# Two transpositions of a top-k attention layer moved from TensorE to VectorE's 32x32 block transposes and transfers

## The chip, the cores and the metric

The program runs on one core of one Trainium2 chip. The metric is the device time of one execution, in microseconds (us). Before the change it is 2491.27 us, the median of three runs (2487.93 to 2491.57). The core's engines are TensorE (PE, with its weight loads PEld), VectorE (DVE), ScalarE (ACT), GpSimd (POOL) and SyncE (SP), each with an instruction queue of its own that it works through in order. Sixteen DMA engines carry the transfers that SP, ACT and POOL issue.

## The reference

Two layers in float32, on 8 images (batches) of 512 channels and 1024 positions (tokens):

```python
# layer 0: group norm, 8-head attention over 1024 tokens, projection, residual
x = _L0_conv_ref(x, ...)
# layer 1
q, kk, v = wq @ xf, wk @ xf, wv @ xf                # [B, 512, 1024]
importance = nan_to_num(sum(xf * xf, axis=1))       # one number per token
_, idx = top_k(importance, 256)
q_sel, k_sel, v_sel = q[idx], k[idx], v[idx]        # 256 rows of 512
q_sel, k_sel = layer_norm(q_sel), layer_norm(k_sel)
attn = softmax(clip(q_sel @ k_sel.T * 512**-0.5, -80, 80))
out = v.at[idx].set(attn @ v_sel)                   # 256 tokens are replaced
return x + wo @ out
```

## The kernel before

Layer 0 fills the first four fifths of the time. Its output, the input of layer 1, lies in DRAM (`x1_dram`). Layer 1 works image by image. Wo is multiplied into Wv ahead of it (`w["vo"]`), so a token's value is its row of the output already. For an image `b` the steps are:

- `load_x1` (L204): four transfers of 512 KB bring the image, channels on the partitions.
- `row` (L245), `square` (L250), `keep_row` (L255), `put` (L258): for each of 8 blocks of 128 tokens TensorE transposes four 128x128 tiles into PSUM. ScalarE sums the squares into the importance, copies the rows to SBUF and issues their transfer to `x_dram`.
- `finite` (L261), `spread_row` (L269), `imp` (L277): the importance, a number per partition, is spread over all partitions by 8 TensorE transposes and two copies of ScalarE.
- `count` (L281), `place` (L328), `pick` (L336), `holder` (L344), `who` (L353): VectorE counts for each token how many are ahead of it (its place), and a small product finds which token holds each of the 256 places.
- `vo` (L306), `vkeep` (L314), `vput` (L325): 32 products of 128 tokens by 512 channels (8 blocks times 4 channel tiles) give all values. ScalarE copies them to the tile `V` and issues their transfer to `v_dram`.
- `gather` (L359, steps getx and getv), `selt`, `selk`, `qk` (L401), `stats`, `root`, `normal` (L424), `normt`, `scale` (L449), `score`, `clip`, `exp`, `inv`, `probt`, `probk`, `att`, `attk` (L521), `attput` (L527): the attention of the 256 chosen tokens, down to a transfer to `a_dram`. Only the last image takes `vsel` and `vselk` (L372 to L383), which compute the chosen values again rather than gather them.
- `fetch` (L533): eight indirect transfers of POOL write the attended rows over those tokens of `V` that were chosen; an index past 255 moves nothing.
- `back` (L546), `residual` (L541), `add` (L555): TensorE transposes `V` back, 32 tiles of 128x128 per image; VectorE adds the image's x, read once more from DRAM, and SP sends the sum out in eight transfers of 256 KB.

The order of all this is written out by hand in the strings `BATCH` (one round, repeated) and `END` (the last rounds), one word per step: `vo3` is `vo(b, 3)`, each `+` is one image ahead of the round's, each `-` one behind. Every engine's queue gets its instructions in the order of that list, those that issue transfers too. `EARLY` names the steps of image 0 that are done in layer 0's last units, through `token_rows` (L904), `token_values` (L916), `importance` (L1096), `count_first` (L1106), `begin_layer1` (L1135) and `finish` (L1157).

Of the kernel before, what the change touches and what calls it, by code (L numbers as in the profile page):

```python
# [9 lines left out]
F32 = mybir.dt.float32  # L10
BF16 = mybir.dt.bfloat16
I32 = mybir.dt.int32
AF = mybir.ActivationFunctionType
ALU = mybir.AluOpType
# [4 lines left out]
P = 128  # L19
# [20 lines left out]
BLOCKS = 2 * HALF // BLOCK  # L40
ET = mybir.EngineType
# [17 lines left out]

BATCH = """  # L60
vkeep6- square1 inv-- put4 put2 holder- add3--- keep1 square2 back4--- att0-- att1-- who-
row6 put1 row0 add4--- row7 keep0 back7--- square0 row3 keep6 attk0-- put0 square3 vo0 row5
vput7- square6 getx- vput4- attk1-- keep3 square7 square5 add7--- vput5- back6--- keep7
finite vo1 attput-- add6--- vput0- vkeep0 keep5 selt1- selt0- spread1 spread0 fetch1-- imp1 imp0
count2 fetch0-- put6 count5 vo3 count7 vkeep1 selk1- selk0- qk1- count6 count3 qk0-
fetch5-- qk2- vput6- vput3- stats0- stats1- vput2- qk3- root0- stats2- root2- fetch2-- norm0-
vkeep3 put5 norm2- vput1- root1- vo4 vkeep4 stats3- fetch3-- norm1- vo2 root3- back0--
fetch6-- fetch4-- norm3- fetch7-- normt1- normt0- count4 vkeep2 add0-- put3 put7 back5--
normt2- normt3- scale2- scale3- row4+ add5-- back1-- scale1- count0 back2-- vo5 scale0-
count1 square4+ keep4+ place score0- score1- clip- back3-- vo6 vkeep5 pick0 add1-- exp- vo7  # L70
getv- add2-- pick1 row2+ probt- vkeep7 row1+ probk- keep2+
"""
END = """
vput2-- put4- vkeep6-- row3- add3---- square2- holder-- att1--- back4---- row0- who-- inv---
put2- row7- square1- keep1- attk1--- att0--- getx-- square3- keep3- keep0- keep7- put1- put3-
put7- row5- back6---- attk0--- row6- square7- back7---- square6- add4---- square0- square5-
keep5- keep6- put0- vput5-- vo1- put5- selt1-- finite- vkeep1- spread1- add6---- add7----
selk1-- selt0-- spread0- imp1- imp0- attput--- count1- vo0- row6 row2 vput7-- selk0-- count6-
keep6 keep2 row1 square2 count0- count2- vput6-- count7- row0 count3- vkeep0- square1 keep1
put1 vput1-- qk0-- row7 qk1-- put6- square0 put2 stats1-- qk3-- stats0-- count5- put6 keep7  # L80
square6 vo7- put7 root1-- vput1- fetch5--- row4 root0-- norm0-- qk2-- keep0 stats3--
fetch3--- count4- vo6- place- square4 vkeep7- keep4 norm1-- square7 root3-- stats2-- row3
vput0- vkeep6- vo4- normt1-- root2-- norm3-- normt0-- vput0-- row5 keep3 fetch1--- vput4--
vput3-- norm2-- vkeep4- scale1-- normt2-- put3 normt3-- scale0-- fetch2--- pick1- scale2--
square5 square3 keep5 put5 vo2- fetch0--- pick0- holder- finite spread0 scale3-- put4 vkeep2-
imp0 getv-- fetch6--- spread1 who- imp1 score0-- back2--- count4 score1-- fetch7--- count2
clip-- exp-- count3 vput2- back0--- count7 getx- vput4- count6 put0 add0--- vo3- count0
fetch4--- probt-- vkeep3- probk-- inv-- add2--- att0-- att1-- attk1-- attk0-- selt1- selt0-
selk1- selk0- attput-- count5 fetch6-- count1 qk3- place stats3- pick0 back3--- back4---
vput6- add4--- root3- pick1 back1--- qk2- fetch4-- qk0- fetch0-- norm3- add3--- fetch2--  # L90
vput7- back7--- stats2- stats0- holder fetch3-- fetch1-- qk1- who vput3- add7--- root0-
root2- add1--- back5--- norm2- getx add5--- back6--- vo5- normt3- stats1- norm0- fetch7--
root1- fetch5-- norm1- normt2- vkeep5- add6--- normt0- normt1- back2-- scale0- scale3-
scale2- back5-- back7-- vput5- add2-- back1-- add1-- selt1 back6-- back3-- scale1- add7--
add5-- score0- add6-- back0-- selt0 score1- selk1 add3-- clip- selk0 qk2 exp- stats2 back4--
qk1 probt- probk- stats1 getv- add0-- qk0 qk3 att1- root2 root1 norm2 norm1 stats0 inv-
stats3 add4-- root0 attk1- vo1 att0- root3 norm3 vkeep1 norm0 attk0- normt3 normt2 normt0
attput- scale3 normt1 fetch5- scale0 scale1 fetch7- fetch6- vo0 vkeep0 scale2 score1 fetch1-
score0 clip vsel1 fetch4- vo3 exp vselk1 vsel0 vselk0 probt fetch0- probk fetch2- vkeep3 vo6
att1 inv fetch3- att0 vo7 vkeep6 vo2 back0- attk1 back2- back4- attk0 vkeep7 back3- attput  # L100
vkeep2 add3- add0- back5- vo4 fetch7 fetch3 vo5 vkeep4 add2- back1- back7- fetch2 back6-
fetch0 fetch1 add4- add1- fetch6 add7- add5- back2 back4 add4 add6- back0 back6 fetch4 vkeep5
add0 fetch5 back3 back7 add2 back1 add6 back5 add3 add7 add1 add5
# [15 lines left out]
def attention_then_topk_attention(  # L119
# [23 lines left out]
    x1_dram = [dram.tile([P, CT, N], F32, tag=f"x1d{b}", name=f"x1d{b}") for b in range(B)]  # L143
# [25 lines left out]

    xp = ctx.enter_context(tc.tile_pool(name="xp", bufs=1))  # L170
# [6 lines left out]
    a_dram = [dram.tile([TOP, C], F32, tag=f"sa{b}", name=f"sa{b}") for b in range(B)]  # L177

# [25 lines left out]
    def load_x1(b):  # L204

        if b % 2 and b < B - 1:
            x1[b] = [qk_tile(tag, i, f"x1_{b}_{tag}{i}") for tag in "qk" for i in range(2)]
        else:
            if b == B - 1:
                t = pools["x2"].tile([P, CT, N], F32, tag="x2", name=f"x1_{b}")  # L210
            else:
                t = xp.tile([P, CT, N], F32, tag="x1", name=f"x1_{b}")
            x1[b] = [t[:, c, :] for c in range(CT)]
        for c in range(CT):
            nc.sync.dma_start(x1[b][c], x1_dram[b][:, c, :])

    def load_layer1():

        t = wide.tile([P, CT, 3 * C], F32, tag="w3", name="w1")
        for i, (name, src) in enumerate((("q", wqT), ("k", wkT), ("vo", None))):  # L220
            w[name] = t[:, :, ts(i, C)]
        load_x1(0)
        for name, src in (("q", wqT), ("k", wkT)):
            nc.sync.dma_start(w[name], src.rearrange("(k p) o -> p k o", p=P))
# [18 lines left out]


    def row(b, j):  # L245
        pt = bank(("pt", b, j))
        for c in range(CT):
            nc.tensor.transpose(pt[:, ts(c, P)], x1[b][c][:, ts(j, P)], ident)

    def square(b, j):  # L250
        norm = get("r1", ("norm", b), [P, NB], "norm", 2)
        sq = keep_pool.tile([P, C], F32, tag="sq", name=f"sq_{b}_{j}", bufs=1)
        nc.scalar.activation(sq, tiles["pt", b, j], AF.Square, accum_out=norm[:, j : j + 1])

    def keep_row(b, j):  # L255
        nc.scalar.copy(get("r1", ("xT", b, j), [P, C], "xT", XT), tiles["pt", b, j])

    def put(b, j):  # L258
        nc.scalar.dma_start(x_dram[b][ts(j, P), :], tiles["xT", b, j])

    def finite(b, _):  # L261
# [4 lines left out]
        col = get("r1", ("col", b), [P, NB], "col", 2)  # L266
        nc.vector.scalar_tensor_tensor(col, norm, F32_MAX, fin, ALU.is_le, ALU.mult)

    def spread_row(b, j):  # L269
        pi = bank(("pi", b, j))  # L270
        for i in range(NB // 2):
            nb = j * (NB // 2) + i
            nc.tensor.transpose(
                pi[:, ts(i, P)], tiles["col", b][:, nb : nb + 1].broadcast_to([P, P]), ident
            )

    def imp(b, j):  # L277
        t = get("rp", ("imp", b), [P, N], "imp", 1)
        nc.scalar.copy(t[:, ts(j, HALF)], tiles["pi", b, j])
# [26 lines left out]
    def vo(b, j):  # L306
        pv = bank(("pv", b, j))
        for k in range(CT):
            nc.tensor.matmul(  # L309
                pv, x1[b][k][:, ts(j, P)], w["vo"][:, k, :],  # L310
# [3 lines left out]
    def vkeep(b, j):  # L314
        if ("V", b) not in tiles:
            if b % 3:
                tiles["V", b] = pools["up"].tile([P, NB, C], F32, tag=f"V{b % 3}", name=f"V_{b}")
            else:
                tiles["V", b] = xp.tile([P, CT, N], F32, tag="x0", name=f"V_{b}").rearrange(
                    "p c (a n) -> p (c a) n", n=C  # L320
                )
        V = tiles["V", b]
        nc.scalar.copy(V[:, j, :], tiles["pv", b, j])

    def vput(b, j):  # L325
        nc.scalar.dma_start(v_dram[b][ts(j, P), :], tiles["V", b][:, j, :])

    def place(b, _):  # L328
# [4 lines left out]
        nc.vector.tensor_copy(get("rp", ("at", b), [P, NB], "at", 4, mybir.dt.uint32), t)  # L333
# [38 lines left out]
    def vsel(b, rb):  # L372

        pv = bank(("sv", b, rb))
        for k in range(CT):
            nc.tensor.matmul(  # L376
                pv, tiles["selT", b][:, k, ts(rb, P)], w["vo"][:, k, :],
                start=(k == 0), stop=(k == CT - 1),
            )
# [894 lines left out]
```

## Time and profile before

| what | us |
|---|---|
| median of three runs | 2491.27 |
| the profiled execution, its own time | 2489.56 |
| its span, first to last instruction | 2487.9 |
| busy time in the span: PE, DVE, ACT, POOL | 2437.7, 1963.3, 1414.8, 1160.7 |
| start of layer 1's first tile on PE (image 1's rows, L248) | 2020.7 |
| last matrix instruction of image 0's to 7's values (L309), end | 2475.4 |
| data moved from 2020 us on | 84.49 MB |

A profile line of the groups reads: line of the code, engine, operation, output<-inputs by the program's names, shapes, count; then the group's busy time and the mean of one in ns; then the engine's idle time before it. PE's instructions are pipelined and a single one's duration overlaps the next one's; what one costs is read from a run of them in the chain of waits, which lists what ended last as start, duration, engine, tile, line and count. A 128x512 product in float32 is two instructions.

### The profile page before, as it was taken

The numbers are of one execution on the slowest core, as the hardware profiler recorded it, in microseconds if no ns is written. First come the engines' busy times: TensorE is split into PE (matmuls) and PEld (weight loads), VectorE is DVE, ScalarE is ACT, GpSimd is POOL, SyncE is SP. The second block draws the span as 40 slices with busy tenths as digits, with TensorE's granted clock in tenths as the row PEclk, the third lists the DMA queues.
The fourth block names the chain that finished last, engine by engine and source line by source line (L and its number), as shares of the span: only waits on it lengthen the run. The fifth ranks groups of instructions, "written<-read, shape, count | busy, mean of one in ns | idle before, by whom it ended". The sixth has DMA issues, their size and how long they took to land. (4 is left out here: it accounts for less than half of the span.)

```text
span 2487.9 us, 27088 instructions
## 1 busy us (share of the span) xinstructions
PE 2437.7 (98%) x9164; PEld 1076.4 (43%) x9164; DVE 1963.3 (79%) x2946; ACT 1414.8 (57%) x1828; POOL 1160.7 (47%) x557
## 2 busy tenths in 40 slices
PE   7999999999999999999999999999999999999998
PEld 3434444444444444444444444444433345555554
DVE  4789987998898889888988898888777566666683
ACT  2567755665666566655765676567656533333421
POOL 0555644665465555545664565455555501111122
PEclk9999999999999999999999999999999999999999
DMA  3002011111211121112011201111213343566553
GB/s 142 15 26 73 30 56 51 69 35 56 84 31 43 56 79 41 43 60 77 26 47 56 77 26 49 59 39 35 89 52 106 123 161 136 209 211 240 188 198 106
DMA packets 108234, 205.24 MB, mean 82 GB/s; under 512 B 19114, under 2 KB 19370, under 8 KB 108096
## 3 DMA queue, kind: packets, MB, share of 16 engines
q1 hardware_dynamic: 82432, 159.95, 19.0%
q10 hardware_dynamic: 18144, 31.48, 3.4%
q0 software_dynamic: 7520, 12.09, 1.7%
q8 instruction: 72, 1.18, 0.2%
q14 instruction: 66, 0.54, 0.1%
HBM read 146.29 MB, written 69.73 MB: 87 GB/s over the span
## 5 line engine op out<-in xcount | busy, mean ns | idle before, releaser
L1014 POOL TENSOR_TENSOR es<-es,e 128x1024 f32<-128x1024 f32 x384 | 912.0, 2375 | 30.1
L955 ACT COPY e<-sc 128x1024 f32<-128x1024 f32 x512 | 505.6, 1013 | 389.4 <-PE sc L947 241.3
L1006 DVE TENSOR_TENSOR e<-e,ns 128x1024 f32<-128x1024 f32 x512 | 594.0, 1212 | 2.0 <-ACT ns L1002 2.0
L1014 POOL TENSOR_TENSOR es<-e,e 128x1024 f32<-128x1024 f32 x64 | 152.0, 2375 | 884.8 <-ACT e L1009 884.8
L1009 ACT ACTIVATE e<-e 128x1024 f32<-128x1024 f32 x512 | 529.1, 1055 | 31.6 <-DVE e L1006 9.8
L961 DVE TENSOR_TENSOR high<-sc,high 128x1024 f32<-128x1024 f32 x384 | 468.9, 1221 | 90.0 <-ACT e L955 50.3
L947 PE MATMUL sc<-q,k 64*128 64x512 f32 x2048 | 510.4, 616 | 5.3 <-ACT e L955 3.2
L1022 PE MATMUL av<-e,v 128*64 128x512 f32 x2048 | 469.4, 600 | 3.5 <-ACT e L1009 2.0
L750 PE MATMUL g<-x,wqkv 128*128 128x512 f32 x992 | 458.8, 605 | 3.4 <-ACT v L780 1.7
L947 PEld LDWEIGHTS sc<-q,k 64*128 64x128 f32 x2048 | 175.3, 185 | 283.6 <-issue 151.3
L750 PEld LDWEIGHTS g<-x,wqkv 128*128 128x128 f32 x992 | 178.3, 189 | 274.8 <-issue 229.9
L1022 PEld LDWEIGHTS av<-e,v 128*64 128x64 f32 x2048 | 136.1, 137 | 320.6 <-issue 257.5
L771 PE MATMUL g<-wqkv,x 128*128 128x256 f32 x976 | 227.0, 386 | 1.3 <-DVE pb L834 1.3
L789 PE MATMUL g<-o,wp 128*128 128x512 f32 x456 | 210.9, 605 | 0.8
L771 PEld LDWEIGHTS g<-wqkv,x 128*128 128x128 f32 x976 | 180.4, 190 | 69.7 <-issue 43.3
L1051 DVE RECIPROCAL rs<-rs 128x256 f32<-128x256 f32 x64 | 112.1, 1751 | 68.4 <-ACT rs L1045 68.4
L534 POOL DMA_INDIRECT V<-sa,at x64 | 64.2, 1003 | 155.2 <-DMA sa<-att 52.7
L789 PEld LDWEIGHTS g<-o,wp 128*128 128x128 f32 x456 | 81.9, 189 | 118.2 <-issue 91.3
L309 PE MATMUL b_pv<-w,x 128*128 128x512 f32 x256 | 114.1, 592 | 0.0
L405 PE MATMUL b_pp<-w,selT 128*128 128x512 f32 x256 | 112.5, 593 | 0.8 <-ACT selT L396 0.7
L961 DVE TENSOR_TENSOR high<-sc,e 128x1024 f32<-128x1024 f32 x64 | 78.1, 1220 | 37.5 <-ACT e L955 37.5
L363 POOL DMA_INDIRECT sel<-sx,who x16 | 16.1, 1007 | 191.0 <-DMA out_dram<-y 72.1
(177 smaller groups left out, 1993.6 us busy)
## 6 DMA issues: line engine op xcount, KB each, us to landing
nb<-negd SPq DMA_DIRECT2D x128, 256.0 KB
x<-in_x_dram SPq DMA_DIRECT2D x32, 512.0 KB
ri<-rsd SPq DMA_DIRECT2D x128, 128.0 KB
sx<-xT ACTq DMA_DIRECT2D x64, 256.0 KB
xr<-in_x_dram SPq DMA_DIRECT2D x58, 256.0 KB
x1d<-xr SPq DMA_DIRECT2D x58, 256.0 KB
sv<-V ACTq DMA_DIRECT2D x56, 256.0 KB
y<-x1d SPq DMA_DIRECT2D x48, 256.0 KB
```

Of the source, the lines that this page charges most:

```text
L309: nc.tensor.matmul(pv, x1[b][k][:, ts(j, P)], w["vo"][:, k, :], start=(k == 0), stop=(k == CT - 1),)
L405: nc.tensor.matmul(pp, tiles["selT", b][:, k, ts(rb, P)], w["qk"[which]][:, k, :], start=(k == 0), stop=(k == CT - 1),)
L750: nc.tensor.matmul(pq, wqkv[:, k, ts(ot, P)], hs[b][:, k, ts(hf, HALF)], start=(k == 0), stop=(k == CT - 1),)
L771: nc.tensor.matmul(pv[:, ts(j, 2 * P)], hs[b][:, k, ts(2 * part + j, P)], wqkv[:, k, 2 * C + hm * 2 * P : 2 * C + (hm + 1) * 2 * P], start ...
L789: nc.tensor.matmul(po, wp[:, k, ts(mt, P)], os[b * NPAIR + k][:, ts(hf, HALF)], start=(k == 0), stop=(k == CT - 1),)
L947: nc.tensor.matmul(sc[:, hh, :], ks[p][r, ts(j, P)], qs[p][r, ts(hf, HALF)], start=True, stop=True,)
L955: nc.scalar.copy(raw[t, j], banks["s", t, j])
L961: nc.vector.tensor_tensor(high[t], banks["s", t, j], raw[t, 0] if j == 1 else high[t], ALU.max)
L1006: nc.vector.tensor_tensor(raw[t, j], raw[t, j], high[t], ALU.add)
L1009: nc.scalar.activation(raw[t, j], raw[t, j], AF.Exp, scale=QK_SCALE)
L1014: nc.gpsimd.tensor_add(sums[t], raw[t, 0] if j == 1 else sums[t], raw[t, j])
L1022: nc.tensor.matmul(avs[t][HD * hh : HD * hh + HD, :], vs[p // 2][:, j, (p % 2) * P + HD * hh : (p % 2) * P + HD * hh + HD], e[:, hh, :], s ...
```

## The change

`x1` is now loaded with the channels interleaved: a tile's partitions hold 32 channels of each quarter. `turn` transposes 32x32 blocks of it on VectorE, 16 instructions of 128x256 per image, and `rput` (16 transfers of 32 partitions) puts the blocks together in `x_dram`. `rget` reads the rows back, into the tile `R` in which the output rows will be formed; a partition now holds four consecutive tokens, so `vo` takes every fourth column of `x1` as its stationary operand (`tokens_of`). The importance is spread by a transfer to DRAM and two from it (`nput`, `nget`), the places likewise get into the new token order (`atput`, `atget`). `V` is no longer kept: POOL adds it to the rows in `R` (step resid), `attk` adds the chosen row of x, `fetch` overwrites in `R`, and `back` transposes `R` in 16 block transposes of 128x256, which `store` sends out in 16 transfers of 32 partitions. Reading x a second time, `residual` and `add` go. The layer norm's factors are computed for two row blocks at once (`var`, `factor`), and `normal` and all of `scale` are ScalarE's. `vsel` and `vselk` go. Image 0 still has its rows turned by TensorE. `BATCH` and `END` are new lists, and loads are steps of them.

```diff
+Q = P // BLOCK
+J = HALF // P
...
 BATCH = """
...
+load2++ vkeep4 count0 place scale3- pick1 vkeep3 resid5 scale1- normt0- load0++ vo1+ scale0-
+vkeep1+ score0- vkeep6+ resid4 pick0 score1- holder vo0+ vput3 load3++ square5+ who getx vo2+
+square7+ square6+ square4+ clip- rget0+ exp- probt- load1++ selt1 probk- vput4 inv- selt0
+att1- att0- turn2++ selk1 selk0 square0+ resid3 store0-- store1-- square2+ atget- attk1-
+square1+ square3+ vkeep0+ attk0- finite+ turn3++ qk2 qk3 turn0++ resid6+ stats2 nput+ vkeep2+
+stats3 resid1+ vput0+ var1 qk0 root1 qk1 attput- nget+ rput2++ turn1++ factor1 vo7+ fetch7-
+vput1+ stats0 fetch4- norm2 count7+ fetch5- vput6+ norm3 vkeep7+ rput3++ vo3+ fetch6- count2+
+atput stats1 var0 rput0++ root0 vo5+ fetch1- fetch0- normt2 rput1++ vkeep5+ vput5+ count4+
+normt3 factor0 fetch3- fetch2- count1+ resid2+ vput2+ back2- back3- store2- back0- scale2
+vput7+ count3+ store3- vo4+ back1- rget1++ norm0 getv norm1 count5+ resid7+ normt1 count6+
+vo6++ resid0+
 """
 END = """
...
+normt1 scale0 scale1 attput- store1-- back3-- fetch4- store0-- score1 resid5 fetch3- score0
+fetch6- clip exp probt probk fetch2- store2-- store3-- fetch0- fetch5- inv att1 att0 attk1
+fetch7- attk0 resid7 fetch1- back2- attput fetch3 back0- back1- back3- fetch1 fetch0 store2-
+fetch2 store1- store0- fetch5 fetch6 fetch4 store3- fetch7 back1 back0 store1 back2 store0
+back3 store2 store3
 """
...
+        for a in range(Q):
+            nc.sync.dma_start(
+                x1[b][c][ts(a, BLOCK), :],
+                x1_dram[b][a * P + c * BLOCK : a * P + (c + 1) * BLOCK, :],
+            )
...
+    def tokens_of(t, j):
+
+        return t.rearrange("c (h p j) -> c h j p", h=NH, j=J)[:, j // J, j % J, :]
...
+    def turn(b, u):
+
+        t = piece(("T", b, u)).rearrange("p (s c q) -> p c s q", c=CT, q=BLOCK)
         for c in range(CT):
...
+            nc.vector.transpose(
+                t[:, c], x1[b][c][:, ts(u, N // 4)].rearrange("p (s r) -> p s r", r=BLOCK)
+            )
+
+    def rput(b, u):
+        t = tiles["T", b, u].rearrange("p (s n) -> p s n", n=P)
+        d = x_dram[b][ts(u, N // 4), :].rearrange("(s r) c -> r s c", r=BLOCK)
+        for a in range(Q):
+            nc.sync.dma_start(d[:, :, ts(a, P)], t[ts(a, BLOCK)])
+
+    def rget(b, h):
+        nc.sync.dma_start(
+            rows(b)[:, ts(h, J), :],
+            x_dram[b][ts(h, HALF), :].rearrange("(p j) c -> p j c", j=J),
+        )
...
+    def nput(b, _):
+        nc.sync.dma_start(
+            place_of(n_dram[b]), tiles["fin", b].rearrange("p (h j) -> p h j", h=NH)
+        )
+
+    def nget(b, _):
+
+        nc.sync.dma_start(
+            get("rp", ("imp", b), [P, N], "imp", 1), n_dram[b].unsqueeze(0).to_broadcast([P, N])
+        )
+        nc.sync.dma_start(
+            get("r1", ("col", b), [P, NB], "col", 2), n_dram[b].rearrange("(a p) -> p a", p=P)
+        )
...
-                pv, x1[b][k][:, ts(j, P)], w["vo"][:, k, :],
+                pv, tokens_of(x1[b][k], j), w["vo"][:, k, :],
...
+    def residual(b, j):
+        r = rows(b)[:, j, :]
+        nc.gpsimd.tensor_add(r, r, tiles["V", b, j])
...
+    def atput(b, _):
+        nc.sync.dma_start(at_dram[b].rearrange("(a p) -> p a", p=P), tiles["to", b])
+
+    def atget(b, _):
+        t = get("rp", ("at", b), [P, NB], "at", 4, U32)
+        nc.sync.dma_start(t.rearrange("p (h j) -> p h j", h=NH), place_of(at_dram[b]))
...
+        nc.scalar.activation(
+            r[:, rb, :], tiles["pp", b, i], AF.Identity,
+            bias=tiles["sh", b, which][:, rb : rb + 1],
+            scale=tiles["nf", b, which][:, rb : rb + 1],
         )
...
+        nc.vector.scalar_tensor_tensor(
+            t[:, rb, :], tiles["pa", b, rb], tiles["den", b][:, rb : rb + 1],
+            tiles["sel", b][:, rb, :], ALU.mult, ALU.add,
         )
...
+        h, g = divmod(i, 2)
+        t = piece(("Y", b, i)).rearrange("p (s k j) -> p j s k", k=BLOCK, j=J)
+        for j in range(J):
+            nc.vector.transpose(
+                t[:, j],
+                rows(b)[:, h * J + j, ts(g, C // 2)].rearrange("p (s q) -> p s q", q=BLOCK),
+            )
+
+    def store(b, i):
+        h, g = divmod(i, 2)
+        t = tiles["Y", b, i].rearrange("p (s n) -> p s n", n=P)
+        d = out[b, ts(g, C // 2), ts(h, HALF)].rearrange("(s q) n -> q s n", q=BLOCK)
+        for a in range(Q):
+            nc.sync.dma_start(d[:, :, ts(a, P)], t[ts(a, BLOCK)])
...
+            for name, bufs in (("tp", 4), ("rp", 2), ("up", 1), ("mp", 2)):
...
-                for j in range(2):
-                    count_first(j)
...
-                    count_first(2 + i)
+                    count_first(i)
...
+                for j in range(len(outs), NB):
+                    count_first(j)
```

## The prediction

> **What bounds the kernel now.** I read first the page's table of slices, then a table of busy time over five stretches of layer 1, then the chain of waits, then the groups by form.
>
> ```profile
> PE   7999999999999999999999999999999999999998
> ...
> DMA  3002011111211121112011201111213343566553
> ```
>
> ```profile
> 2100.00:2200.00 100.00, 99.42 (x405) 57.06 (x404) 66.50 (x204) 35.13 (x81) 16.01 (x16) 1.00 0.53 178
> 2200.00:2300.00 100.00, 98.99 (x379) 54.65 (x377) 63.11 (x199) 38.05 (x87) 22.02 (x22) 1.00 0.68 243
> 2300.00:2400.00 100.00, 98.42 (x412) 56.15 (x411) 76.89 (x246) 38.53 (x90) 24.16 (x24) 1.00 0.55 185
> 2400.00:2488.00 88.00, 78.62 (x305) 45.67 (x303) 39.29 (x90) 19.07 (x38) 17.93 (x18) 0.99 0.40 138
> ```
>
> The columns of the second are the stretch, its length, busy us of PE, PEld, DVE, ACT and POOL, granted clock, DMA share and GB/s. PE works 98 to 99 us of each 100 at clock 1.00, DVE 63 to 77, the DMA engines about 0.6. TensorE sets the pace. Only the last stretch has a hole. The chain of waits agrees and gives unit prices:
>
> ```profile
> 2419.11 0.44 PE b_ppt L503 x4
> ...
> 2428.13 3.43 PE b_pv L309 x8
> ...
> 2441.91 3.43 PE b_sv L376 x8
> ...
> 2475.44 0.45 PE b_po L550 x4
> 2475.89 0.02 issue
> 2475.91 6.07 DVE x L558 x10
> ```
>
> Four transposes of 128x128 cost 0.44 us, 0.109 each; eight instructions of 512 columns (four products) 3.43, 0.43 each. After the last transpose 12.0 us follow without PE.
>
> **TensorE, removed.** The groups by form from 2020 us on count what goes:
>
> ```profile
> L550 PE MATMUL b_po<-ident,V 128*128 128x128 f32 x256 | 34.9, 273 | 2.6 <-DMA V<-sa,at 2.6
> ...
> L248 PE MATMUL b_pt<-ident,x 128*128 128x128 f32 x128 | 17.6, 273 | 0.0
> ...
> L273 PE MATMUL b_pi<-ident,col 128*128 128x128 f32 x56 | 7.9, 277 | 1.6 <-DVE col L267 1.0 <-ACT xT L256 0.6
> L376 PE MATMUL b_sv<-w,selT 128*128 128x512 f32 x16 | 7.2, 593 | 0.0
> ```
>
> L248 has two more groups (x_q, x_k) of 48. That is 256 + 224 + 56 = 536 transposes by 0.109, 58.4 us, and vsel's 16 by 0.43, 6.9: **65.3 us**. Image 0's rows stay. An image of the steady rounds took 64 (vo) + 32 (qk) + 8 (att) instructions by 0.43, 16 of score by 0.216, 100 transposes by 0.109 and 0.5 for holder, 59.6 us; without 72 transposes it is 51.7. Nothing is added to PE.
>
> **vo's strided stationary operand.** Its columns now lie 16 bytes apart. No weight load of the trace is strided. A load takes 190 ns and hides behind a product of 430, so up to 430 costs nothing. The nearest row is VectorE's L987, which reads in steps of 128 bytes:
>
> ```profile
> L972 DVE STREAM_TRANSPOSE mT<-high 128x512 f32<-128x512 f32 x100 | 70.7, 707 | 1.7
> L973 DVE TENSOR_REDUCE quarter<-mT 128x16 f32<-128x512 f32 x100 | 68.6, 686 | 3.5
> ...
> L985 DVE STREAM_TRANSPOSE four<-quarter 32x32 f32<-32x32 f32 x200 | 40.0, 200 | 3.8
> ...
> L987 DVE TENSOR_REDUCE neg<-four 32x32 f32<-32x128 f32 x50 | 18.4, 368 | 1.7
> ```
>
> By the slope of the transposes, (707 - 200)/480 = 1.06 ns an element, 128 contiguous elements reduce in 686 - 384 x 1.06 = 279 ns; 368 is 0.7 ns an element more. A load would take 190 + 90 = 280: hidden. [...] If the load took 600 ns, 448 loads by 170 would be 76 us. I follow the row: 0, between 0 and 76. Below nothing is excluded, for a product's rate is not in question.
>
> **VectorE.** A 128x256 block transpose is 200 + 224 x 1.06 = 437 ns; 32 per image, 14.0 us. back writes in steps of 16 bytes, 0.7 x 256 x 16 = 2.9 us by L987, between 0 and twice that. Away go eight adds by 0.684 (5.5), four normalisations by 0.809 (3.2), four scales by 0.537 (2.1) and half of the small factor steps (1.6). attk gets a third operand: 0.749 us now, and L796 of the same form takes 0.74, so 0. An image had 42 us (the rows of layer 1, each by its count per image): 42 - 12.4 + 16.9 = 46.5, 90% of PE's 51.7. It is hidden, but hardly has slack left; without that cover it costs each us itself.
>
> **ScalarE and GpSimd.** ScalarE loses keep and imp (8 x 0.588, 2 x 0.6) and gains normal and scale (4 x 0.6, 4 x 0.565): less than before, 35 busy in 100. GpSimd gets eight adds, by half of L1014's 2375 ns 1.2 us each, beside 12 indirect transfers by 1.0 and 0.3 for issue: 25 us per image, hidden. The adds stand before the fetches in its queue and wait for the rows (rget) and vkeep.
>
> **SyncE's queue.** Issues per image go from 21 to 56 (16 loads, 16 rput, 16 store, 8 more). One took 0.32 to 0.54 us: 18 to 30 us of 51.7. The new waits stand in this queue: rget waits for rput to land, nget for nput, atget for atput, a trip of about 3 us each (sa<-att landed in a median of 3.1). Behind nget stand rput and store, which free the four buffers that turn and back share; so a late importance stops VectorE some 10 us later. This is cover, not slack: I put it in the slip below.
>
> **The DMA engines.** The new load, rput and store are 6.3 MB per image in copies of 32 partitions; the rest (rget, vput at 2.1 MB, five of 0.52) 6.8 MB. Before: 51.19 MB in 240 us from 2100 on at a share of 0.613, 348 GB/s while busy. No copy of 32 partitions of that size is in the trace. The nearest is two copies to 64 partitions (ri) followed by one of 128 (x1d), from 905.5 to 911 us:
>
> ```profile
> DMA  0000000000245449696999897622100000000000
> GB/s 0 0 0 0 0 0 0 0 0 0 89 149 209 164 179 209 104 209 164 238 268 358 328 358 283 238 104 89 60 15 0 0 0 0 0 0 0 0 0 0
> ```
>
> A slice is 0.14 us. The narrow ones run at 104 to 209, about 170 GB/s, the wide one at up to 358. Scaled by partitions, 32 would run at 85: 74 us per image, and with 6.8/0.348 = 20 us the DMA engines would need 94. [...] Between 38 (all at 348) and 94 I take 53 to 57, the upper with the row's 170. The 512-byte runs of rput and store and the 4-byte runs of nget and atput (some 2,000 per image) are in no row; a few us, either side of this.
>
> So PE at 51.7, DMA at 53 to 57 and VectorE at 46.5 lie together in queues that can't overtake. I add a slip of 2.5 us per round, for six rounds 15 us.
>
> **The start.** Image 0's counts (8 by 2.05 us) stood ready when layer 1 began: place at 2020.6. Now they wait for nput and nget (about 6 us after the squares near 1994), and the five residual sums, the division and image 1's turns (7.0) stand on VectorE before place too: 2001 + 16.4 + 4.4 + 7 + 2.8 (place, pick) = 2032. PE has only two blocks of vo (6.9 us) before holder, till about 2025: **+7.5**.
>
> **The end.** vo of the last image, which filled PE until 2475, now comes early in END. The last image's scale, clip, exp and probk have nothing beside them: 2.3 + 2.75 + 1.4 + 0.6 = **+7** on PE. After the last att: attk 0.75, attput 3.5, eight fetches by 1.3, landing 3, two backs 3.5, four issues 1.5 and landing 3 make 26 us, where 12 stood: **+14**.
>
> **The sum,** against the profiled span: 2487.9 - 65.3 + 7.5 + 7 + 14 + 15 = 2466. Around the span lay 1.7 us (2489.56), and the median is 1.7 higher still: **2469 us**, 0.9% faster.
>
> **The rivals.**
> 1. *TensorE alone sets the pace* (no slip): 2454. For it: no other engine's own sum reaches 51.7, and loads of x1 moved up to 400 GB/s. Against: three resources within 15%.
> 2. *Forecast*, slip 1 to 5 us: 2460 to 2485.
> 3. *No change*: slip about 6: within 2486 to 2496.
> 4. *The quarter copies make DMA the bound*, slower. Place: rput and load in SyncE's queue, ahead of turn. It decides from a round of 51.7 + 6 = 57.7 us; at 170 GB/s and 5 us for short runs a round is 62, and 2454 + 6 x 10.3 = 2516. For it: 53 to 57 is a busy time, and so far the engines' share was 0.6. [...]
> 5. *Strided access*: vo's loads above 430 ns or back at double price: 2500 to 2530.
> 6. The change not doing what it says: the steps removed are gone from the lists, so hardly.
>
> **How the numbers follow.** 0.20, 0.36, 0.07, 0.27, 0.10. About 0.2%, 5 us, is what a measurement tells from no change. Faster: 0.56. Same: 0.07. Slower: 0.37. The range runs from 2442 (rival 1 with the end's waits half hidden) to 2530, which leaves out slower copies than 170 GB/s; the likeliest case's own is 2460 to 2485.
>
> **What would show it.** Right: no L248 or L550 among PE's groups after 2025 us, vo's eight still at 3.43, b_pv's weight loads under 430 ns, block transposes near 440, PE above 92% in 2100 to 2300, a hole of about 7 us near 2025 and 25 us after the last att. Wrong: PE near 85% there with SyncE waiting for transfers and a DMA share above 0.9 (rival 4); vo's eight longer, or back well above 600 ns (rival 5); a start or end that costs double.

## The result, and the profile after

| | median, us | runs | ratio to before |
|---|---|---|---|
| before | 2490.64 | 2487.93 to 2491.57 | |
| after | 2546.7 | 2542.96 to 2547.97 | 1.0224 [1.0207, 1.0242] |

The change made the kernel 2.2% slower; its profiled execution took 2547.55 us with a span of 2545.8. The table of busy time over stretches, with the columns of the one shown before:

```profile
2100.00:2200.00 100.00, 88.59 (x251) 53.23 (x251) 67.35 (x193) 36.66 (x79) 36.44 (x34) 0.95 0.80 201
2200.00:2300.00 100.00, 81.27 (x253) 51.61 (x253) 66.39 (x181) 35.48 (x75) 33.85 (x30) 0.90 0.83 211
2300.00:2400.00 100.00, 89.81 (x264) 54.69 (x263) 62.81 (x196) 34.72 (x72) 37.81 (x35) 0.93 0.77 186
```

TensorE works 81 to 90 us of 100, where it worked 98 to 99, at a granted clock of 0.90 to 0.95, where it was 1.00. No other engine comes near 100 in its place: VectorE has 63 to 67, the DMA engines 0.77 to 0.83. So the work did go from TensorE, and more than that came back as waiting. From one holder to the next (read from who, which follows it) the rounds from the second on take 65.2, 64.4, 63.7, 65.6 and 65.5 us. Before, the four from the second on took 58.2 to 60.6; the forecast had 51.7 and 2.5 of slip.

The chain of waits of after shows how such a round ends (start, us, what):

```profile
2267.64 4.88 issue
2272.52 0.08 DVE junk L344
...
2290.77 0.50 PE b_pn L394 x13
2291.28 9.61 PE b_pv L352 x16
```

The 4.88 us of "issue" lie within one instruction of VectorE, the count's third (L344, 0.35 us else), which reads two operands from SBUF. It ends when four additions of GpSimd (resid), which run back to back beside it, are done:

```profile
2267.17 5.42 DVE L344 SCALAR_TENSOR_TENSOR junk<-imp,col,before 128x128 f32<-128x128 f32 x1
2267.49 4.94 POOL L365 TENSOR_TENSOR R<-R,V 128x512 f32<-128x512 f32 x4
```

VectorE then still has four backs, four counts, place and pick to do, and TensorE waits until 2290.77 for the picks (47.8 us in five such waits between 2050 and 2450). After the hole it runs at half clock at first (granted 0.50 until 2295): two vo blocks take 9.61 us, not 2 x 3.43. What VectorE itself waited for between 2050 and 2450 (total, times, longest):

```profile
DVE T L278 <- DMA x<-x1d: 44.1, 4, 15.0
DVE T L278 <- DMA x_q<-x1d: 33.4, 4, 11.9
DVE Y L583 <- DMA sx<-T: 32.8, 6, 10.0
```

Turn waits for the loads of x1, and back for the buffers that rput has yet to empty: late transfers, at a DMA share of 0.8. The experiments had to tell why they are late.

### The profile page after: what moved, and what is told of

Read it like the earlier page. It is cut to its first block, busy times and chain, and to the rows that moved or that the text cites. A ratio compares the mean times of both kernels' runs of the same rounds, so it can differ in the third digit from the quotient of the medians.

```text
span 2545.8 us, 26349 instructions
## 1 busy us (share of the span) xinstructions
PE 2410.2 (95%) x8604; PEld 1084.7 (43%) x8604; DVE 1986.3 (78%) x2978; ACT 1416.3 (56%) x1802; POOL 1244.9 (49%) x623
## 4 chain that ended last, share of the span: by engine, by line
PE 80%; DVE 7%; DMA 5%; issue 3%; POOL 2%; ACT 2%; SPq 1%; POOLq 0%; ACTq 0%; DVEq 0%
PE sc L972 17%; PE g L771 17%; PE av L1047 17%; PE g L792 8%; PE g L810 7%; PE b_pv L352 3%; PE b_pp L438 3%; DMA sv<-V 2%; POOL es L1039 2%; PE den L1062 1%; PE last L810 1%; DVE Y L583 1%; PE b_pa L553 1%; DVE e L1031 1%; DVE junk L340 1%
## 5 line engine op out<-in xcount | busy, mean ns | idle before, releaser
L365 POOL TENSOR_TENSOR R<-R,V 128x512 f32<-128x512 f32 x64 | 80.5, 1275 | 112.0 <-ACT sq L297 60.5
L572 POOL DMA_INDIRECT R<-sa,at x64 | 64.3, 1004 | 100.1 <-DMA sa<-att 83.3
L583 DVE STREAM_TRANSPOSE Y<-R 128x256 f32<-128x256 f32 x128 | 63.4, 621 | 46.1 <-DMA sx<-T 32.8
```

## First experiments: queue, width, runs

Theory 1: SyncE's and ScalarE's transfers share eight completion semaphores, handed out in the order of the list of steps (in the trace of after the transfers of both queues count up the same eight, 100 to 106 and 108), and each transfer waits until the one eight places before it has landed. In the trace SyncE waits 100.8 us before rputs and 53.4 us before loads for sv<-V, a V row that ScalarE writes. Theory 2 (rival 4 of the prediction): copies of 32 partitions are slow. Theory 3: GpSimd's additions hold up VectorE.

**vput_pool**: the rows of V by another queue.

```diff
-        nc.scalar.dma_start(rows_at(v_dram[b], j), tiles["V", b, j])
+        nc.gpsimd.dma_start(rows_at(v_dram[b], j), tiles["V", b, j])
```

> The rows of V go to memory by GpSimd's queue instead of ScalarE's; same bytes, same number of transfers, and nothing left out. Theory 1, coupled queues: SyncE's and ScalarE's transfers share eight completion semaphores in the order of the list, so a load, rput or store in SyncE's queue waits until a V row that TensorE has not yet computed has landed. Out of that order, the 100.8 + 53.4 us in which SyncE waits for sv<-V go, a round falls from 64.4 us to 55 to 58, and the time to 2490 to 2510. Theory 2, the rate of copies of 32 partitions: the bytes are as before, so 2540 to 2550, and SyncE waits as long for something else. Theory 3, GpSimd in VectorE's way: eight more issues of about 1 us per image on GpSimd make it slower, 2550 to 2570.

Measured: 2539.66, ratio 1.0208 [1.0191, 1.0225]. SyncE no longer waits for sv<-V, but for the backs (44.4 us before rget) and the importance (34.6). Theory 1 is at most a few us.

**wide**: load, rput and store as one transfer each.

```diff
-        for a in range(Q):
-            nc.sync.dma_start(d[:, :, ts(a, P)], t[ts(a, BLOCK)])
+        d = x_dram[b][ts(u, N // 4), :].rearrange("(p m) c -> p (m c)", m=2)
+        nc.sync.dma_start(d, tiles["T", b, u])
```

(load and store likewise.)

> Load, rput and store each as one transfer of 128 partitions with runs of 4 KB: the same bytes, a quarter of the transfers. The rows and the output then lie in another order, so the values are not the reference's. Theory 2 (narrow copies or short runs cost rate): DMA share falls to about 0.6, a round to 52 to 55 us, time 2470 to 2490. Theory 1 (coupled queues): 36 transfers fewer per image, but the ones left still wait for V's rows: a round of 58 to 62, 2510 to 2530. Theory 3: no change, 2540 to 2550.

Measured: 2518.12, 1.0117 [1.0100, 1.0134]; rounds of 60 to 63 us from the second on, DMA share still 0.73 to 0.78 in the three stretches of 100 us. The time fell by some 27 us, half of what was lost, but neither the share nor the round fell as theory 2 said. The time lies in theory 1's range; yet SyncE's waits for sv<-V, which theory 1 expected to stay, are gone from its list.

**long_runs**: rput and store in four narrow copies, each with its own 64 or 32 contiguous rows as the destination.

> rput and store keep their four copies of 32 partitions, but write runs of 4 KB instead of 512 bytes; rows and output lie in another order, so the values are not the reference's. Theory 2 with the short runs as its cause: DMA share falls below 0.7, time 2490 to 2510. Theory 2 with the narrow copies as its cause, and theory 1: 2535 to 2550.

Measured: 2540.56, 1.0206 [1.0189, 1.0223]. The short runs of rput and store are not the cause.

**wide_four**: four transfers each, cut along the columns (`[:, ts(a, N // Q)]`) instead of the partitions.

> Load, rput and store each as four transfers of 128 partitions and 128 KB, with runs of 1 KB: the number and size of the transfers as they were, only their width changes; rows and output lie in another order, so the values are not the reference's. Theory 2 with the width as its cause: 2475 to 2500, as the kernel with one wide transfer each. Theory 1, where the number and the order of transfers count: 2535 to 2550.

Measured: 2529.66, 1.0157 [1.0140, 1.0174], between both expectations.

## Second experiments: order, buffers, additions

**back_late**: in the list, `clip- rget0+` becomes `clip- back0-- back1-- rget0+`, and back0- and back1- are left out but in the last steady round.

> In the steady rounds the two backs of an image's first half stand after the next holder instead of before it; nothing else moves. Theory 4, bunched VectorE: between the last qk and the holder VectorE has stats, factor, eight counts, four backs, place and pick, 34 us, and TensorE only 26 us; between the holder and the end of qk it is the other way round, so each round lasts the longer halves, whatever the sums are. Two backs fewer in the long half are 5 us per round, and the hole before the holder (47.8 us in 2050 to 2450) shrinks by as much, with 1 to 2 us of low clock behind it: 2505 to 2520. Theories 1 and 2 (transfers): VectorE's order doesn't matter, 2540 to 2550.

Measured: 2544.78, 1.0203 [1.0184, 1.0222]. The wait for pick did shrink, from 47.8 to 11.9 us; in its place TensorE waits 37.8 us in probt for exp, and the rounds from the second on take 56.8, 64.6, 64.7, 65.1 and 74.7 us. The hole moves with the order; the late transfers behind it remain.

**v_ring_11**:

```diff
-        nc.scalar.copy(get("r1", ("V", b, j), [P, C], "xT", XT), tiles["pv", b, j])
+        pool, tag, bufs = ("rp", "V1", 7) if b and j % 2 else ("r1", "xT", XT)
+        nc.scalar.copy(get(pool, ("V", b, j), [P, C], tag, bufs), tiles["pv", b, j])
```

> V's rows of images 1 to 7 go to eleven buffers (four and seven) instead of four; nothing else changes. Theory 5, the ring of V: ScalarE's vkeep waits until V's row of four places before has landed and been added, and everything behind it in ScalarE's queue waits too (sd, norm, scale); with eleven buffers ScalarE's 24 us of waits for sv<-V go, SyncE's waits shrink since V's rows leave sooner, and the time falls to 2515 to 2530. Theories 2 and 4: 2540 to 2550.

Measured: 2541.63, 1.0195 [1.0178, 1.0212]. ScalarE's wait in vkeep is gone from its list, but SyncE's 99.7 and 57.8 us stayed.

**no_residual**: `nc.gpsimd.tensor_add(r, r, tiles["V", b, j])` left out.

> The residual addition of V to the rows is left out, so the output is not the reference's. Theory 3, GpSimd in VectorE's way: the counts' third instruction goes from 680 back to 351 ns and nf from up to 1.7 us to 0.2, 4 us per round, and V's buffers come free sooner: 2510 to 2525. Theories 1, 2 and 4: 2538 to 2550.

Measured: 2539.18, 1.0185 [1.0168, 1.0202]. The count's third instruction goes from a mean of 574 ns back to 352, as before the change. The mean misleads: the median is 352 ns in after too, but two of its 64 take 5.80 and 5.42 us, each beside four additions in a row, and here none takes more than 0.39. The time falls by 7 to 10 us, about as much as these two. The mechanism is real and small here.

**one_load**: one transfer per load step, to the right places.

```diff
+        nc.sync.dma_start(
+            x1[b][c], x1_dram[b].rearrange("(a c r) n -> c a r n", a=Q, c=CT)[c],
+        )
```

> Each of the four load steps is one transfer to 128 partitions that reads four runs of 32 rows, instead of four transfers to 32 partitions; the same bytes to the same places, twelve transfers fewer per image. Theories 1 and 2: SyncE's waits before loads (53.4 us) shrink to a quarter, turn2 no longer waits 12 us per round for its load: 2525 to 2538. Theory 4: the wait of turn lies in the half in which VectorE has time, 2540 to 2550.

Measured: 2585.94, 1.0367 [1.0349, 1.0385], a miss. Where VectorE waits for these loads (132 us) the DMA share is at times only 0.27 to 0.49, at 106 to 155 GB/s; in after it is 0.77 to 0.83 over 100 us. My reading, which no run tests by itself, is that a transfer of this form keeps only a part of the engines busy. Since the form of the transfers changed along with their number, the run does not tell what the number is worth.

## What all of them had in common

Every one of these kernels issues atput once per image. In after, within 5 to 10 us behind each of the eight, 29 to 68 packets, most of them of 2 and 4 KB, take over 0.7 us each, the longest 6.4 us; the median of all packets of 2 KB from 2050 on is 0.084. The table of stretches of after, 2 us each (the last two columns are DMA share and GB/s):

```profile
2259.00:2261.00 2.00, 2.00 (x6) 1.40 (x5) 1.96 (x7) 0.26 (x1) 1.70 (x2) 1.00 0.83 227
2261.00:2263.00 2.00, 2.00 (x6) 1.51 (x5) 1.90 (x8) 0.20 (x1) 1.39 (x3) 1.00 0.98 114
2263.00:2265.00 2.00, 2.00 (x6) 1.40 (x6) 1.97 (x4) 0.00 (x0) 1.97 (x2) 1.00 0.25 21
2265.00:2267.00 2.00, 2.00 (x12) 1.60 (x11) 1.86 (x8) 0.62 (x2) 1.55 (x2) 1.00 0.87 43
2267.00:2269.00 2.00, 2.00 (x6) 1.40 (x6) 1.96 (x3) 2.00 (x4) 1.97 (x3) 1.00 0.83 34
2269.00:2271.00 2.00, 2.00 (x9) 1.47 (x8) 2.00 (x1) 1.31 (x4) 2.00 (x2) 1.00 0.48 43
2271.00:2273.00 2.00, 2.00 (x6) 1.40 (x6) 2.00 (x3) 0.53 (x2) 1.43 (x2) 1.00 0.77 287
```

A packet counts in the 2 us in which it starts, with its whole time; so a share can pass 1, or be low behind a long packet.

SyncE issues atput (st<-to) at 2259.67: 1024 writes of 4 bytes. From 2263 on the engines, at shares up to 0.87, move 21 to 43 GB/s until 2271, then 287 again. Three rows of V, which ScalarE issues at 2266 and 2267, send one packet before 2271. All eight atputs of after are followed by such a stretch, in the second of up to 120 GB/s. The trace of before has none: where its packets are slow, from 2022 to 2026, 173 and 211 GB/s are moved. The nget read of col has 1024 runs of 4 bytes too and is followed by no such stretch, nor are the 256 writes of 16 bytes of nput. Theory 6: these single writes freeze the transfers.

**at_runs**: the same values, written in 128 runs of 32 bytes and sorted when they are read.

```diff
-        nc.sync.dma_start(at_dram[b].rearrange("(a p) -> p a", p=P), tiles["to", b])
+        nc.sync.dma_start(at_dram[b].rearrange("(p a) -> p a", p=P), tiles["to", b])
...
-        nc.sync.dma_start(t.rearrange("p (h j) -> p h j", h=NH), place_of(at_dram[b]))
+        d = at_dram[b].rearrange("(r j h a) -> h a r j", r=BLOCK, j=J, h=NH)
+        for h in range(NH):
+            nc.sync.dma_start(t[:, ts(h, J)], d[h])
```

> The place of each token is written to memory as 128 runs of 32 bytes instead of 1024 runs of 4 bytes, and read back by two transfers in the order that fetch needs (1024 reads of 4 bytes); values and everything else as they were. Theory 6, the freeze: after each of these writes all transfers stand nearly still for 7 to 10 us (packets of 2 KB take over 0.7 us instead of 0.085, at a DMA share near 1 and 16 to 45 GB/s), and what waits for a transfer then, V's rows, rput, stores, the backs, moves back by as much. Without the single writes the freezes go, eight of them, six in the steady rounds: a round of 55 to 58 us, 2485 to 2505. Theories 1, 2, 4 and 5: 2540 to 2550.

Measured: 2522.9, 1.0125 [1.0107, 1.0144]: right in kind, 18 us short of the expectation. The write is issued at 2252.41 here:

```profile
2253.00:2255.00 2.00, 2.00 (x6) 1.49 (x5) 1.93 (x9) 0.20 (x1) 1.69 (x2) 1.00 0.74 188
2255.00:2257.00 2.00, 2.00 (x12) 1.47 (x11) 1.83 (x6) 0.59 (x1) 1.68 (x3) 1.00 0.12 32
2257.00:2259.00 2.00, 2.00 (x6) 1.52 (x6) 2.00 (x4) 1.19 (x3) 1.74 (x2) 1.00 0.78 276
```

No freeze: the 32 GB/s in the middle come with a share of 0.12, so the engines have nothing to do, and 276 follow.

**at_double**: the write of 4-byte runs issued twice.

> The place of each token is written twice, one transfer of 1024 runs of 4 bytes after the other. Theory 6: each freeze lasts twice as long, 15 to 20 us, and the round grows by 7 to 10 us: 2585 to 2625. Theories 1 to 5: one small transfer more in SyncE's queue, 2545 to 2555.

Measured: 2612.54, 1.0473 [1.0456, 1.0491]. That is 2.5% of 2490, 62 us more than after, for eight more such writes: 7.8 us each. Taking the first eight away gave 25 us, 3.1 each. Theory 6 stands from both sides, though what a freeze costs depends on what waits beside it.

**at_runs_vput_pool** and **at_runs_ring_back**: the earlier edits on top.

> The place in runs of 32 bytes, and V's rows through GpSimd's queue. With theory 6 as the main cause and theory 1 as a smaller one (7 us by itself): 5 to 15 us below the kernel with the runs alone, 2475 to 2495. If the waits for V's rows were only another face of the freeze, no gain over the runs alone.

Measured: 2526.6, 1.0128 [1.0111, 1.0145], no gain.

> The place in runs of 32 bytes, V's rows in eleven buffers and two backs after the next holder. If the freeze hid theories 4 and 5 when they were tried alone, they come out now: 10 to 25 us below the kernel with the runs alone, 2465 to 2490. If they are no cause: within 5 us of it.

Measured: 2538.7, 1.0184 [1.0167, 1.0201], slower than the runs alone. Theories 4 and 5 bring nothing here, with the freeze or without it.

## The rest: the width of the copies

**at_runs_wide**: both edits.

> The place in runs of 32 bytes, and load, rput and store each as one transfer of 128 partitions with runs of 4 KB; rows and output lie in another order, so the values are not the reference's. If the freeze (24 us by itself) and the narrow copies (28 us by itself) are two causes side by side: 2485 to 2500. If both act through the same late transfers: 2510 to 2520, as each alone. If with both gone no transfer is late any more and TensorE sets the pace: 2455 to 2475.

Measured: 2478.39, 0.9950 [0.9933, 0.9967]; 0.5% faster than before, with values that are not the reference's. By the ratios taking away the freeze alone is worth 1.0% (25 us), the narrow copies alone 1.1% (27 us), both 2.7% (68 us). With wide copies the freeze is worth 42 us, 5.2 per write: while one makes transfers late, taking away the other shows only in part. Its stretches:

```profile
2100.00:2200.00 100.00, 98.10 (x290) 61.96 (x289) 78.53 (x231) 40.71 (x86) 39.83 (x36) 0.98 0.65 223
2200.00:2300.00 100.00, 96.23 (x298) 60.29 (x297) 74.92 (x216) 38.72 (x82) 43.53 (x40) 1.00 0.70 240
2300.00:2400.00 100.00, 97.68 (x298) 62.28 (x297) 72.68 (x223) 39.83 (x86) 33.94 (x30) 0.98 0.60 201
```

TensorE is back at 96 to 98, the clock near 1, and six rounds take 329 us; the forecast had 325. The price of a narrow copy, in the same table of after (narrow load, then narrow rput):

```profile
2227.00:2229.00 2.00, 1.93 (x15) 1.22 (x16) 1.37 (x5) 1.95 (x5) 0.75 (x1) 0.50 1.04 236
...
2275.00:2277.00 2.00, 2.00 (x6) 1.40 (x6) 1.47 (x4) 1.70 (x4) 0.00 (x0) 1.00 0.89 237
```

and of at_runs_wide (wide load, then wide rput):

```profile
2198.00:2200.00 2.00, 2.00 (x11) 1.74 (x11) 1.90 (x11) 1.94 (x6) 0.00 (x0) 1.00 1.04 401
...
2228.00:2230.00 2.00, 2.00 (x6) 1.05 (x5) 1.93 (x9) 0.00 (x0) 1.51 (x2) 1.00 1.04 406
```

With the engines busy (shares of 0.89 to 1.04) they move 236 GB/s in copies of 32 partitions and some 400 in copies of 128. The rows of load show it best: SyncE issues rput's copies of 128 KB one per 0.51 us, 255 GB/s at most, so its pace may hold rput down too. For 6.3 MB per image that is 27 against 16 us, an estimate from the two rates. (The first row also shows the half clock after a hole.)

**at_runs_long** and **at_runs_wide_four**, to tell width from runs and number:

> The place in runs of 32 bytes; rput and store as four copies of 32 partitions each, with runs of 4 KB instead of 512 bytes; rows and output lie in another order, so the values are not the reference's. If the short runs are what makes the narrow copies dear: 2490 to 2500 of the 2523 without the change and the 2478 of wide transfers. If width or number: 2515 to 2525.

Measured: 2521.07, 1.0102 [1.0077, 1.0126].

> The place in runs of 32 bytes; load, rput and store as four copies of 128 partitions and 128 KB with runs of 1 KB; rows and output lie in another order, so the values are not the reference's. If the width makes the difference: 2480 to 2490, near the 2478 of one wide transfer. If the number of transfers (eight semaphores, 0.4 to 0.5 us per issue): 2510 to 2525.

Measured: 2482.85, 0.9955 [0.9938, 0.9971]. Four wide transfers with runs of 1 KB are as good as one, so the number is not it; four narrow ones with runs of 4 KB (rput and store; load had them already) are as bad as with 512 bytes, so the runs are not it. What is left is the width.

**at_runs_vput4** and **at_runs_vput_all**, theory 1 once more; in the list `vput3 load3++` becomes `vput3 vput4 load3++`, and in the second every vput follows its vkeep.

> The place in runs of 32 bytes, and the word vput4 moved from behind exp and probk to behind vput3, where V's row 4 has long been kept; nothing else. Theory 1, coupled queues: load1 shares its semaphore with that transfer, so that SyncE's 49.5 us of waits before loads and VectorE's 75 us of waits in turn for x go, and a round falls by 5 us or more: 2490 to 2505. If the loads are late for their rate: 2518 to 2526, no change.

Measured: 2516.69, 1.0108 [1.0092, 1.0125]. SyncE's wait for V before loads fell from 49.5 to 6.5 us as said, but came back before rputs (21.1 to 66.7) and stores (20.8 to 43.6); a gain of some 4 us by the ratios, which their intervals do not separate from none.

> The place in runs of 32 bytes, and every vput moved to directly behind its vkeep. Theory 1: no load, rput or store waits for a row that has long been computed; 2480 to 2500. Against it: now ScalarE itself can be held by a store or load of SyncE eight transfers before, 2515 to 2530.

Measured: 2526.56, 1.0154 [1.0132, 1.0176], no gain.

**at_runs_vput4_load**, with the right values throughout: layer 0 writes in the order in which layer 1 reads, and load is one wide transfer.

```diff
-                    nc.sync.dma_start(x1_dram[b][ts(mt, P), ts(hf, HALF)], xr)
+                    d = x1_dram[b].rearrange("(c a r) n -> a c r n", c=CT, a=Q)[mt]
+                    nc.sync.dma_start(d[:, :, ts(hf, HALF)], xr)
```

> All values as they were: the place in runs of 32 bytes, vput4 ahead, and layer 0 writes x1 with its channels in the order in which layer 1 loads them, so that each load is one transfer of 128 partitions. Loads are a third of the bytes and of the transfers that wide copies change, so a third of 44 us below the 2517 with vput4 ahead: 2500 to 2508. If loads are the transfers that VectorE waits for (75 us in turn): 2485 to 2500. If each write of layer 0 that now goes to four runs holds up its end: 2510 to 2520.

Measured: 2490.86, 0.9996 [0.9989, 1.0003]: the loads were the transfers that VectorE waited for (turn's waits fall from 62.9 to 32.4 us), and wide loads alone bring 26 of the 38 us between at_runs_vput4 and at_runs_wide. This is level with before, not better. No run has rput and store as one wide transfer with the right values: in this form a row's four quarters lie on partitions 32 apart. No version with the right values beat before.

## Why the prediction was wrong

**The step that failed** is the one on the DMA engines, in two terms. First: "the 4-byte runs of nget and atput (some 2,000 per image) are in no row; a few us, either side of this." No stretch of slow transfers follows the reads of nget; each atput, 1024 writes, is followed by 5 to 10 us in which nearly no transfer moves (21 to 43 GB/s in the table above). That cost 25 us of 2547 (at_runs), 42 beside wide copies, and eight more such writes cost 62. Second: "I add a slip of 2.5 us per round." The slip was 7.4 in the first round (59.1 - 51.7) and 12.0 to 13.9 in the five others, 73 us in place of 15. The prediction named such a stop ("a late importance stops VectorE some 10 us later") and put it into those 2.5 us. I had added the three queues' busy times beside each other and found that they just fit, but a late load stops VectorE's queue at turn, the counts behind it, TensorE at holder, and then the clock (0.50 behind the holes).

**Rival 4** named the place (load and rput ahead of turn) rightly, and gave 2516 with a round of 62. Without the freeze and with narrow copies, at_runs takes 2522.9, its rounds from the second on 60.0 to 64.7; with the freeze it became 2547. Its mechanism was only half right: TensorE's 81 to 90 us of 100 fit its sign (near 85%), but over 100 us the DMA engines' share was 0.77 to 0.83 and not above 0.9; they were not full. The narrow copies make transfers late in queues that can't overtake; they don't fill the engines. Of the busy time of 53 to 57 us per image that I took, the 57 follows from the row's 170 GB/s, and no run shows the 53; the runs showed 236 GB/s for copies of 32 partitions. The busy time was about right (0.80 of 64.4 is 52) partly by luck: at 236 GB/s the same sum gives 27 + 20 = 47 us, an estimate, and packets that hang in the freeze count as busy too (a share of 0.87 at 43 GB/s). I judged by a sum of busy time where lateness decided.

**What was right.** TensorE's removal, 65.3 us: with freeze and narrow copies gone, a round takes 54.8 us (329 / 6), where 51.7 and 2.5 stood. vo's strided weight loads take 311 ns (estimate 280) and stay hidden (24 of vo's instructions in a row take 10.31 us in after, eight 3.44). Turn's transposes take 405 to 420 and back's 621 ns (437, and 437 + 180). After the last att 26.3 us follow (26). Near it was the start, 5 us of later TensorE and 4.6 of waiting for 7.5. The end was put too low: holes of 4.3 us in 2436 to 2476 and 6.9 in 2489 to 2513 stand for 7, and the clock there was 0.89 and 0.90. Of the 9 us that at_runs_wide is above the forecast 4 lie in the rounds, the others outside them.

**Missed:** the prediction called GpSimd's additions hidden. In after they hold up the count's third instruction, which has two operands in SBUF: 5.80 and 5.42 instead of 0.35 us at worst. The record of the 5.42 us begins 0.32 us before the first addition and ends 0.16 us after the last of four in a row; why VectorE waits is not shown. It is not the freeze: in at_runs, which has none, such an instruction takes 6.83 us (at 2382.05). no_residual puts it at 7 to 10 us. And the trip of about 3 us, given as that of sa<-att, is that of fetch's transfers (V<-sa,at in before, a median of 3.1 us to landing); sa<-att took 2.8 to 6.1 us there.

**Open:** why the writes freeze the transfers; whether it is their size or their number, since at_runs changes both; and what the new order by itself is worth, which no run had alone.

## What to carry to other kernels

Before moving work from an engine to transfers, look for two things that a sum of bytes hides: many single writes of a few bytes to memory (eight times 1024 of 4 bytes cost 25 us here; at_runs wrote contiguous runs and sorted when reading) and copies that reach only 32 partitions (236 GB/s here, where copies of 128 moved some 400). And where queues can't overtake, count the wait of the first instruction that needs a late transfer with all that stands behind it; busy times that "just fit" beside each other don't. When single repairs give little, try two together before dropping either.

## What the runs showed of the hardware

In after, each transfer of 1024 writes of 4 bytes is followed by 5 to 10 us of slow transfers; from 2263 to 2271 all queues together move 21 to 43 GB/s. The one of 1024 reads of 4 bytes at 2251.18 is not followed by such a stretch (129, 207 and 342 GB/s in the next 6 us), nor is that of 128 runs of 32 bytes written in at_runs at 2252.41 (32 GB/s at a share of 0.12, then 276). In after a VectorE instruction with two operands in SBUF took 5.42 us instead of 0.35 beside four GpSimd additions in a row. Copies of 32 partitions in flight together moved 236 GB/s (load, runs of 4 KB) and 237 (rput, 512 bytes) in after, and copies of 128 some 400 in at_runs_wide (401 and 406). In the holes of 8.7 to 10.3 us before holder in after, TensorE's granted clock fell to 0.50, and it was still 0.50 in the first 4 us behind them.
